# A Mamba, attention and mixture-of-experts block: one scan for both tiles of a second chunk, a convolution on one engine, and the last attention in two halves

## The chip, the cores and the metric

The kernel runs on one core of a Trainium2 chip. A core has five engines that run side by side, each through its own instructions in order: PE (TensorE, matrix products), DVE (VectorE), ACT (ScalarE), POOL (GpSimd) and SP (SyncE, which here only issues DMAs). DMA queues move data between HBM and the core's memory. The metric is the device time of one execution in microseconds; the median of several executions is compared.

## The reference

The input is x of shape 8 x 256 x 32 x 32: 8 batches of 1024 tokens with 256 channels. Cut to what matters here, layer 0 is this, with layer norms and residual additions around it:

```python
xm, z = split(xn @ W_in)                    # 512 channels each
xm = silu(causal_conv(xm, conv_w, 4 taps) + conv_b)
dt, Bm, Cm = split(xm @ W_x)
dt = softplus(dt @ W_dt + b_dt)             # [tokens, 512]
A = -exp(A_log)                             # [512, 16 states]
for t in tokens:                            # h: [512, 16]
    h = exp(dt[t] * A) * h + (dt[t] * xm[t]) * Bm[t]
    y[t] = sum over states of h * Cm[t]
y = (y + xm * D_param) * silu(z)
x = x + y @ W_out
x = x + gelu(layernorm(x) @ W1 + b1) @ W2 + b2
```

Layer 1 is attention with 8 heads of 32 channels over the 1024 tokens of a batch, with a bias per key column and head, and then a mixture of experts: the mean of a batch's tokens is routed, its two best of 8 experts (256 to 512 to 256 channels with GELU) are applied to all its tokens and added with weights, and a layer norm follows.

## The kernel before

**Tiles and steps.** A batch has two chunks of 512 tokens, 16 chunks in all. In a chunk the 512 inner channels are four tiles of 128 partitions, taken as two halves of two tiles each. The recurrence runs along the free dimension: for one state and one tile of channels, the scan instruction computes h over 512 tokens from the decays da_all and the inputs hb. A chunk has 16 states x 2 halves = 32 steps; the whole kernel has 512, walked by one loop (L2239). Each step g has four parts, all of them written by hand into the order of the engines' queues:

- `decay` (L891): ACT writes exp(dt * A) for both tiles into da_all, which has two buffers, two steps ahead.
- `inputs` (L908): DVE multiplies dt * xm with the row B, broadcast over partitions (tile bc), into a slot of the set h4 (tile hb), one step ahead. There are 4 slots; from a point in the run, when the weight w_z is no longer needed, its memory is a fifth (L958).
- `scan` (L920): DVE runs the recurrence over hb in place.
- `sums` (L943): DVE multiplies hb with the row C in place, and POOL issues a DMA that adds hb to the half's sum dx in memory (512 KB). The next step that adds to the same dx comes two steps later, and POOL waits for the earlier addition to land.

In the first chunk of a batch (c = 0) one scan instruction runs through both tiles as one row of 1024 elements; the decay of the second tile's first token is zero, so that nothing carries over. After it, POOL copies the last h of both tiles into the tile state. In the second chunk (c = 1) there are two scan instructions of 512 elements, one per tile, which start from the column of state as an operand; the two exponentials for two steps ahead follow one behind each of them.

**The other work** is written as Python generators, which a model of the engines' queues (L60 to L137) resumes when its clock says that their inputs are ready: `advance` (L2129) gives each due stream its turn by the order in URGENT, and where PE would stand idle it emits filler matmuls into unused memory (tile warm). The model's costs are constants in `vec_cost`, `act_cost`, `pe_cost`, `pool_cost`. The streams are:

- `prologue` (L685), the next chunk's xm, dt and dx: the convolution runs on DVE as three operations xm<-xp per tile, or, where CONV is set (chunks 3, 4 and 13), on PE as 16 products cv<-xp per tile; softplus adds its terms by DVE (e<-u) or, where SOFT is set, by POOL's DMAs into dt. FRONT gives the step at which it starts, GATE that of the gate z (`gate_part`, L991).
- `epilogue` (L1039), what follows a chunk's scans: gate, output product, FFN.
- `attention` (L1540), one batch at a time, in 32 units of 4 heads, 512 queries and 128 keys: scores (sc) on PE, exp (pt) on ACT, products with the values (num) on PE. The sum over keys (den) is a PE product too, except in the last batch, where DVE adds pt into the tiles dsum. The last batch's attention needs both chunks, so it starts when the last epilogue has ended.
- `route` (L1717) and `experts` (L1790): a batch's routing, small DVE operations, then indirect DMAs of the chosen experts' weights, issued by POOL (tile g), and the experts' products he and re.

All engine instructions are recorded by one helper, so that in the profile they have the line L98, and all DMAs L95. Operations are told apart by their tiles.

Of the kernel before, what the change touches and what calls it, by code (L numbers as in the profile page):

```python
# [54 lines left out]
def hybrid_kernel(ctx: ExitStack, tc: tile.TileContext, a: dict, out: bass.AP):  # L55
# [46 lines left out]
    def vec_cost(op, out, *ins):  # L102
        n, into = width(out), str(out)
        chained = op == "scalar_tensor_tensor" and vec.into == into
        vec.into = into
        if op == "tensor_tensor_scan":
            return (0.125 if n == CH else 0.07) + n * 2.08e-3
        return (0.2 if n < P else 0.065) + n * 1.04e-3 + 0.2 * chained
# [42 lines left out]
    w_z = load("w_z", [P, KC, DI], a["W_in"].rearrange("(k p) n -> p k n", p=P)[:, :, DI:])  # L151
# [69 lines left out]
    taps = const.tile([P, ND * KW, HD], F32, name="taps")  # L221
# [17 lines left out]
    base1 = const.tile([P, KC], F32, name="base1")  # L239
    base2 = const.tile([P, NF], F32, name="base2")  # L240
# [31 lines left out]
    FRONT = (7, 13, 4, 4, 1, 14, 10, 1, 13, 1, 10, 6, 1, 5, 10)  # L272
    GATE = (20, 4, 30, 30, 22, 7, 30, 18, 28, 25, 5, 28, 30, 30, 12, 26)
    CONV = (0, 0, 0, 1, 1, 0, 0, 0, 0, 0, 0, 0, 0, 1, 0, 0)
    SOFT = (1, 0, 0, 1, 0, 0, 0, 0, 1, 0, 1, 0, 0, 0, 0, 0)
# [274 lines left out]
    set_up, gates_ready, centered_w = [], [], []  # L550
# [43 lines left out]
    def conv_pe(i, xn, mem):  # L594


        c = i % NCH
        while not set_up:
            yield POLL
        xm, xp, ps, ps2 = [], None, None, None  # L600
        for d in range(ND + 1):
            if d < ND:
                if d % 2 == 0:
                    xm.append((yield from mem.take(f"xm_{i}_{d // 2}")))

                ps2 = yield from banks.take(f"xin_{i}_{d}")
                for k in range(KC):
                    pe.matmul(
                        ps2, w_in[:, k, d * P : (d + 1) * P], xn[:, k, :],
                        start=(k == 0), stop=(k == KC - 1),  # L610
                    )
            if d:
                for t in range(KW):
                    for r in range(4):
                        rows = slice(HD * r, HD * r + HD)
                        pe.matmul(
                            ps[rows, :], taps[rows, (d - 1) * KW + t, :], xp[rows, t : t + CH],
                            start=(t == 0), stop=(t == KW - 1),
                        )
                if c < NCH - 1:  # L620
                    act.copy(conv_tail[:, c + 1, d - 1, :], xp[:, CH:])
            yield
            if d:
                h, q = divmod(d - 1, 2)
                act.activation(xm[h][:, q, :], ps, AF.Identity, bias=V("conv_b", d - 1))
                banks.put(ps)
            if d < ND:
                xp = work_pool.tile([P, KW - 1 + CH], F32, name=f"xp_{i}_{d}", tag="xp", bufs=2)
                act.activation(xp[:, KW - 1 :], ps2, AF.Identity, bias=b_in[:, d : d + 1])
                act.copy(xp[:, : KW - 1], conv_tail[:, c, d, :])  # L630
                ps = ps2
            yield
        return xm

    def conv_parked(i, mem):
# [5 lines left out]
        for h in range(NHALF):  # L641
# [11 lines left out]
            if CONV[i]:  # L653
                for q in range(2):
                    d = 2 * h + q
                    ps = yield from banks.take(f"cv_{i}_{d}")
                    for t in range(KW):
                        for r in range(4):
                            rows = slice(HD * r, HD * r + HD)
                            pe.matmul(  # L660
                                ps[rows, :], taps[rows, d * KW + t, :], xps[q][rows, t : t + CH],
                                start=(t == 0), stop=(t == KW - 1),
                            )
                    yield
                    act.activation(xm[h][:, q, :], ps, AF.Identity, bias=V("conv_b", d))
                    banks.put(ps)
                continue
# [17 lines left out]
    def prologue(i: int):  # L685
# [6 lines left out]
        if i < PARK:  # L692
            xn = yield from mem.take(f"xn_{i}")
            yield sp.dma_start(xn, x_v[b, :, :, c * CH : (c + 1) * CH])
            xn = yield from layernorm(mem, banks, xn, xn, f"a{i}", kept=i)
            yield
            me["xn_d"] = dram.tile([P, KC, CH], F32, name=f"xn_d_{i}", tag=f"xn_d_{i}")
            stored = sp.dma_start(me["xn_d"], xn)
            xm = yield from (conv_pe if CONV[i] else conv_dve)(i, xn, mem)
            mem.put(xn, at=max(stored, model.end))  # L700
        else:
            xm = yield from conv_parked(i, mem)
# [6 lines left out]
        def skip_path():  # L709

            for h in range(NHALF):
                dx = me["acc", h] = yield from mem.take(f"dx_{i}_{h}")
                for r in range(2):
                    act.activation(
                        dx[:, r, :], xm[h][:, r, :], AF.Identity, scale=V("D", 2 * h + r)
                    )
# [159 lines left out]
    das, bcs, hbs = {}, {}, {}  # L876
# [14 lines left out]
    def decay(g, q):  # L891
        i, s, h = place(g)
        da = da_all[:, g % 2, q, :]
# [3 lines left out]
        skip = 1 if q and i % NCH == 0 else 0  # L897
        if skip and g % NSTEP < 2:
            act.copy(da[:, :1], zero_c)
        act.activation(  # L900
            da[:, skip:], chunk[i]["dt"][h][:, q, skip:], AF.Exp, scale=neg_a[:, n : n + 1]
        )
# [5 lines left out]
    def inputs(g):  # L908
# [5 lines left out]
        vec.at = max(vec.at, landed)  # L914
        xd = chunk[i]["xd"][h]
        vec.tensor_tensor(hb, xd, bc[:, 0, :].unsqueeze(1).to_broadcast([P, 2, CH]), ALU.mult)
# [3 lines left out]
    def scan(g, q):  # L920

        i, s, h = place(g)
        c = i % NCH
        hb = hbs[g]
        d = 2 * h + q
        done = das.pop((g, q))
        vec.at = max(vec.at, done)
        if c == 0:
            if q:
                both = hb.rearrange("p a t -> p (a t)")  # L930
                vec.tensor_tensor_scan(
                    both, da_all[:, g % 2].rearrange("p a t -> p (a t)"), both, 0.0,
                    ALU.mult, ALU.add,
                )
        else:
            vec.tensor_tensor_scan(
                hb[:, q, :], da_all[:, g % 2, q, :], hb[:, q, :], state[:, s, d : d + 1],
                ALU.mult, ALU.add,
            )
        if q and c < NCH - 1:  # L940
            pool.tensor_copy(state[:, s, 2 * h : 2 * h + 2], hb[:, :, CH - 1])

    def sums(g):  # L943
# [6 lines left out]
        y = hb[:, :, :n]  # L950
        vec.tensor_tensor(y, y, bc[:, 1, :n].unsqueeze(1).to_broadcast([P, 2, n]), ALU.mult)
        model.t = vec.at
        me["landed", h] = pool.dma_start(out=me["acc", h], in_=hb, accum_op=ALU.add)
# [4 lines left out]
    def park():  # L958
# [29 lines left out]
        h4.make = lambda nm, k: w_z if k == H4 else make(nm, k)  # L988
# [50 lines left out]
    def epilogue(i: int):  # L1039
# [20 lines left out]
        for h in range(NHALF):  # L1060
            yield me["landed", h]
            if c < NCH - 1:
                vec.tensor_tensor(
                    me["acc", h][:, :, CH - 1], me["dx_end"][:, 0, h], me["dx_end"][:, 1, h],
                    ALU.add,
                )
            vec.tensor_tensor(y[h], me["acc", h], y[h], ALU.mult)
# [348 lines left out]
    def center():  # L1416
# [17 lines left out]
        for n in range(E * F // (4 * P)):  # L1434
# [3 lines left out]
            mean = work_pool.tile([P, 4], F32, name=f"eW2_m_{n}", tag="r_rows1", bufs=1)  # L1438
# [11 lines left out]
    def expert_constants(pl):  # L1450
        vec.memset(loads_e, 0.0)
        for dst, n, step, mul, add in (
            (rev_e, E, 1, -1.0, float(E)), (base1, KC, P, 1.0, float(E * C)),
            (base2, NF, P, 1.0, float(E * F)),
# [85 lines left out]
    def attention(b: int):  # L1540

        last = b == B - 1
        mem = Owner(t4, 10, 0, NCH + 1) if last else Owner(t4, 6, 0, NCH)
        tn = [chunk[b * NCH + c]["tn"] for c in range(NCH)]
        dsums = []  # L1550
        if last:
            x1 = []
            for c in range(NCH - 1):
                x1.append((yield from mem.take(f"x1l_{c}")))
                sp.dma_start(x1[c], x1_d[b][c])
            x1.append(chunk[b * NCH + NCH - 1]["x1"])
        v = work_pool.tile([P, NT, C], F32, name=f"v_{b}", tag="v")
        for c in range(NCH):
            ps = yield from pairs.take(f"vp_{b}_{c}")
            for q in range(4):  # L1560
                for k in range(KC):
                    pe.matmul(
                        ps[:, q // 2, q % 2 * C : q % 2 * C + C],
                        tn[c][:, k, q * P : (q + 1) * P], wv[:, k, :],
                        start=(k == 0), stop=(k == KC - 1),
                    )
            yield
            vec.tensor_tensor(
                v[:, 4 * c : 4 * c + 4, :].rearrange("p j (h d) -> p j h d", d=HD),
                ps.rearrange("p a (j h d) -> p (a j) h d", h=NH, d=HD),  # L1570
                ecb[:, 4 * c : 4 * c + 4, :].unsqueeze(3).to_broadcast([P, 4, NH, HD]), ALU.mult,
            )
            pairs.put(ps)

# [29 lines left out]
        if last:  # L1604
            for n in range(2):
                dsums.append((yield from mem.take(f"dsum_{n}")))
# [3 lines left out]
        def products(g, c, j, pts):  # L1610
# [5 lines left out]
            for den in range(2):  # L1616
                for r in range(4):
                    h = 4 * g + r
                    if den and last:
# [925 lines left out]
```

## Time and profile before

| what | value |
|---|---|
| median of 5 runs | 3412.2 us (3400.8 to 3417.2) |
| the profiled execution's own time | 3405.1 us |
| its span, first to last instruction | 3403.3 us |
| mean granted clock of PE | 0.961 |
| DVE idle between first and last scan | 141 us of 2954 |
| scan instructions on DVE | 225 + 31 of 1024 elements, 448 + 64 of 512 |
| DMA, mean over the span | 196 GB/s; 8 or 9 tenths busy in most slices of the scan loop |
| dx<-hb, issue to landing | 4.4 / 7.7 / 14.5 us (least, median, most) |

A row of the groups gives line, engine, operation, output<-inputs by the program's names, shapes and count; then busy time and mean ns of one; then the idle time of the engine just before such instructions, and who ended it. In a row of the timeline the first number is the start in us from the span's start, the second the duration. Where several equal instructions follow each other, the timeline shows them as one (x2), and the duration is that of all. An instruction can begin before the one ahead of it on the same engine has ended, so that the distance between two starts says more of a cost than the duration.

### The profile page before, as it was taken

How to read it: one execution, taken by the hardware profiler on the slowest of the kernel's cores; microseconds unless marked ns; L12 is line 12 of the kernel's file. 1: busy time of each engine (PE TensorE's matmuls, PEld its weight loads, DVE VectorE, ACT ScalarE, POOL GpSimd, SP SyncE). 2: the span in 40 equal slices, each digit the busy share in tenths (PEclk: the TensorE clock that was granted, in tenths of full speed). 3: DMA queues.
4: the chain of work that ended last, by engine and by line, in shares of the span. 5: the costliest groups of instructions: out<-in, count | busy, mean ns of one | idle time of the engine just before them, and what ended most of it. 6: DMA issues, size and time to landing. Idle time of an engine off the chain costs nothing. (4 is left out here: it accounts for less than half of the span.)

```text
span 3403.3 us, 44585 instructions
## 1 busy us (share of the span) xinstructions
PE 3145.9 (92%) x16359; PEld 1391.5 (41%) x16359; DVE 2993.8 (88%) x3140; ACT 2466.5 (72%) x3610; POOL 1088.1 (32%) x1072
## 2 busy tenths in 40 slices
PE   8888988999899999999999899999899989999998
PEld 5544443433343334333443344333443343334343
DVE  6989999999989979899989999999999999962561
ACT  4666756678867888687778777787768878864643
POOL 0242134312432235334353245233542353221010
PEclk8989999999999999999999999999999999999999
DMA  4877989989988798889998999799998998972140
GB/s 122 240 197 190 222 214 218 235 205 232 218 212 236 192 216 198 214 208 219 227 244 187 229 226 214 184 215 222 218 240 195 232 220 195 216 170 75 38 97 23
DMA packets 216134, 668.21 MB, mean 196 GB/s; under 512 B 31200, under 2 KB 42592, under 8 KB 215904
## 3 DMA queue, kind: packets, MB, share of 16 engines
q0 software_dynamic: 106112, 373.88, 56.4%
q1 hardware_dynamic: 109792, 291.38, 25.2%
q8 instruction: 130, 2.13, 0.2%
q14 instruction: 100, 0.82, 0.1%
HBM read 269.20 MB, written 92.93 MB: 106 GB/s over the span
## 5 line engine op out<-in xcount | busy, mean ns | idle before, releaser
L98 ACT ACTIVATE da_all<-dt,vecs 128x512 f32<-128x512 f32 (+1 forms) x1024 | 699.6, 717 | 291.1 <-DVE hb L98 247.4
L95 POOL DMA_DIRECT2D dx<-hb x449 | 397.7, 891 | 1379.6 <-DVE hb L98 957.6
L98 DVE TENSOR_TENSOR hb<-xm,bc 128x1024 f32<-128x1024 f32 x449 | 540.5, 1204 | 23.5 <-issue 19.8
L98 DVE TENSOR_TENSOR_SCAN hb<-da_all,state,hb 128x512 f32<-128x512 f32 x448 | 553.1, 1269 | 3.8 <-ACT da_all L98 3.7
L98 ACT ACTIVATE pt<-sc 128x1024 f32<-128x1024 f32 x512 | 494.5, 1018 | 80.1 <-PE sc L98 69.4
L98 DVE TENSOR_TENSOR hb<-hb,bc 128x1022 f32<-128x1022 f32 (+1 forms) x449 | 546.6, 1217 | 0.0
L98 DVE TENSOR_TENSOR_SCAN hb<-da_all,hb 128x1024 f32<-128x1024 f32 x225 | 514.3, 2286 | 8.9 <-ACT da_all L98 8.9
L98 PE MATMUL warm<-mean_c,zero_c 128*128 128x256 f32 x1182 | 374.9, 442 | 49.8 <-ACT z L98 12.7
L98 POOL COPY state<-hb 128x2 f32<-128x2 f32 x225 | 321.0, 1427 | 209.7 <-DVE hb L98 204.6
L98 PE MATMUL sc<-qk,qk 32*128 32x512 f32 x2048 | 336.2, 646 | 21.1 <-ACT pt L98 18.7
L98 PEld LDWEIGHTS warm<-mean_c,zero_c 128*128 128x128 f32 x1182 | 225.6, 211 | 195.2 <-PE warm L98 74.0
L98 PE MATMUL num<-pt,v 128*32 128x512 f32 x2048 | 281.8, 620 | 14.2 <-DVE ot L98 14.2
L98 PE MATMUL den<-pt,ecb 128*32 128x512 f32 x1792 | 239.4, 605 | 0.0
L98 PE MATMUL facc<-fh,w 128*128 128x512 f32 x512 | 233.5, 602 | 5.5 <-ACT pt L98 2.2
L98 PE MATMUL re<-he,g 128*128 128x512 f32 x472 | 219.2, 609 | 19.9 <-ACT sz L98 7.8
L98 PE MATMUL fh<-x_f,w 128*128 128x512 f32 x480 | 228.7, 608 | 7.0 <-DVE x_f L98 2.3
L98 PE MATMUL he<-xe,g 128*128 128x512 f32 x448 | 217.7, 611 | 5.3 <-issue 3.7
L98 ACT ACT_TABLE_LOAD x159 | 204.0, 1283 | 3.5 <-PEq L2532 0.7
L98 PEld LDWEIGHTS sc<-qk,qk 32*128 32x128 f32 x2048 | 99.7, 184 | 200.8 <-ACT pt L98 83.1
L98 PEld LDWEIGHTS facc<-fh,w 128*128 128x128 f32 x512 | 95.4, 192 | 131.4 <-issue 118.2
L98 PEld LDWEIGHTS re<-he,g 128*128 128x128 f32 x472 | 89.4, 195 | 133.5 <-issue 100.8
L98 PEld LDWEIGHTS fh<-x_f,w 128*128 128x128 f32 x480 | 86.9, 191 | 134.6 <-issue 101.8
(422 smaller groups left out, 4697.8 us busy)
## 6 DMA issues: line engine op xcount, KB each, us to landing
dx<-hb POOLq DMA_DIRECT2D x449, 512.0 KB, 7.7
bc<-bc_d SPq DMA_DIRECT2D x256, 512.0 KB
dx<-w_z POOLq DMA_DIRECT2D x63, 512.0 KB, 7.2
dt<-e POOLq DMA_DIRECT2D x36, 512.0 KB, 11.1
dt<-u POOLq DMA_DIRECT2D x30, 512.0 KB, 11.2
xin_d<-z SPq DMA_DIRECT2D x28, 512.0 KB
sz_d<-z SPq DMA_DIRECT2D x28, 512.0 KB
sz<-sz_d SPq DMA_DIRECT2D x28, 512.0 KB
```

The lines of the kernel that those rows point to most:

```text
L95: f(*args, **kw)
L98: return f(*args, **kw)
```

## The change

**Scan.** A slot now has two rows of 513 elements; column 0 holds the state with which the row begins. da_all has the same form, with zeros in column 0, so one instruction of 1026 elements, from an initial value of 0, runs through both rows in both kinds of chunk. In second chunks POOL copies the state into the column; in first chunks POOL clears it, where the slot's column isn't zero already. The inputs' multiply doesn't touch the column. Both exponentials now follow the joined scan. The tile dx has 1026 elements, and the adding DMA carries 1025 of them (the second row's column lies between the two rows).

```diff
     def decay(g, q):
-        da = da_all[:, g % 2, q, :]
+        da = da_all[:, g % 2, q, 1:]
...
-        skip = 1 if q and i % NCH == 0 else 0
-        if skip and g % NSTEP < 2:
-            act.copy(da[:, :1], zero_c)
-        act.activation(
-            da[:, skip:], chunk[i]["dt"][h][:, q, skip:], AF.Exp, scale=neg_a[:, n : n + 1]
-        )
+        act.activation(da, chunk[i]["dt"][h][:, q, :], AF.Exp, scale=neg_a[:, n : n + 1])
...
     def inputs(g):
...
+        if i % NCH:
+            pool.at = max(pool.at, vec.at)
+            pool.tensor_copy(hb[:, :, 0], state[:, s, 2 * h : 2 * h + 2])
+            das[g, 2] = pool.at + 0.3
+            clean.discard(id(hb))
+        elif id(hb) not in clean:
+            pool.at = max(pool.at, vec.at)
+            pool.memset(hb[:, :, 0], 0.0)
+            das[g, 2] = pool.at + 0.3
+            clean.add(id(hb))
         xd = chunk[i]["xd"][h]
-        vec.tensor_tensor(hb, xd, bc[:, 0, :].unsqueeze(1).to_broadcast([P, 2, CH]), ALU.mult)
+        vec.tensor_tensor(
+            hb[:, :, 1:], xd, bc[:, 0, :].unsqueeze(1).to_broadcast([P, 2, CH]), ALU.mult
+        )
...
-    def scan(g, q):
+    def scan(g):
...
+        for q in range(3):
+            vec.at = max(vec.at, das.pop((g, q), 0.0))
+        vec.tensor_tensor_scan(
+            flat(hb), flat(da_all[:, g % 2]), flat(hb), 0.0, ALU.mult, ALU.add
+        )
+        if i % NCH < NCH - 1:
+            pool.tensor_copy(state[:, s, 2 * h : 2 * h + 2], hb[:, :, CH])
...
     def sums(g):
...
-        me["landed", h] = pool.dma_start(out=me["acc", h], in_=hb, accum_op=ALU.add)
+        me["landed", h] = pool.dma_start(
+            out=me["acc", h][:, 1:], in_=flat(hb)[:, 1:], accum_op=ALU.add
+        )
...
-            for q in range(2):
-                scan(now, q)
-                advance()
-                if now + 2 < nsteps and (q or i % NCH):
-                    for r in range(0 if i % NCH == 0 else q, q + 1):
-                        decay(now + 2, r)
+            scan(now)
+            advance()
+            if now + 2 < nsteps:
+                for q in range(2):
+                    decay(now + 2, q)
```

**Convolution, softplus, tables.** `conv_pe`, CONV, the diagonal weights taps and their setup are gone: every chunk convolves on DVE. Two more chunks that count have SOFT set (9 and 15). FRONT and GATE have new values, and `vec_cost` has new constants, so streams fall on other steps.

```diff
-        return (0.2 if n < P else 0.065) + n * 1.04e-3 + 0.2 * chained
+        if op == "tensor_reduce":
+            n = max(n, width(ins[0]))
+        if out.dtype == BF16 and n > CH:
+            return 0.1 + n * 0.535e-3
+        own = 0.2 if n < P else 0.31 if n == P else 0.065
+        if op == "scalar_tensor_tensor" and n == CH:
+            own = 0.13
+        return own + n * 1.04e-3 + 0.2 * chained
...
-    FRONT = (7, 13, 4, 4, 1, 14, 10, 1, 13, 1, 10, 6, 1, 5, 10)
-    GATE = (20, 4, 30, 30, 22, 7, 30, 18, 28, 25, 5, 28, 30, 30, 12, 26)
-    CONV = (0, 0, 0, 1, 1, 0, 0, 0, 0, 0, 0, 0, 0, 1, 0, 0)
-    SOFT = (1, 0, 0, 1, 0, 0, 0, 0, 1, 0, 1, 0, 0, 0, 0, 0)
+    FRONT = (7, 8, 4, 4, 1, 15, 10, 1, 13, 3, 8, 1, 8, 1, 14)
+    GATE = (20, 13, 30, 30, 26, 6, 27, 26, 30, 20, 7, 30, 17, 27, 28, 18)
+    SOFT = (1, 0, 0, 1, 0, 0, 0, 0, 1, 1, 1, 0, 0, 0, 0, 1)
```

**Last attention.** The last batch has a stream of its own, `attention_last`, with an urgency between those of the epilogue and the projections. It makes the values, queries and keys of chunk 14 when that chunk's epilogue has ended, and runs the 8 units of first-half queries and first-half keys; when the last epilogue has ended, it makes those of chunk 15 and runs the other 24. It has four dsum tiles instead of two. The parts that it shares with `attention` have become functions with the same operations (`values`, `scores_of`, `raise_scores`, `quotient`).

```diff
+        yield from operands(0)
+        for n in range(2 * NG):
+            dsums.append((yield from mem.take(f"dsum_{n}")))
+        yield from run_units([(g, 0, j) for g in range(NG) for j in range(NT // 2)])
+        while ("e", b * NCH + 1) not in done:
+            yield POLL
...
+        yield from operands(1)
+        yield from run_units(
+            [(g, 0, j) for g in range(NG) for j in range(NT // 2, NT)]
+            + [(g, 1, j) for g in range(NG) for j in range(NT)]
+        )
```

**Routing.** The row numbers of both weight matrices are computed together (two operations instead of four), and the biases of both layers are picked together:

```diff
         for k in range(2):
-            for rows, base, size, n in ((rows1, base1, C, KC), (rows2, base2, F, NF)):
-                vec.scalar_tensor_tensor(
-                    rows[:, k], first[:, k : k + 1].to_broadcast([P, n]), -float(size), base,
-                    ALU.mult, ALU.add,
-                )
+            vec.scalar_tensor_tensor(
+                rows[:, k], sizes, first[:, k : k + 1], bases, ALU.mult, ALU.add
+            )
...
             for k in range(2):
-                for dst, src, n in ((hbias, "eb1", NF), (obias, "eb2", KC)):
-                    vec.tensor_tensor(
-                        t[:, :n], V(src).rearrange("p (n e) -> p n e", e=E),
-                        oh[:, k].unsqueeze(1).to_broadcast([P, n, E]), ALU.mult,
-                    )
-                    vec.tensor_reduce(dst[:, k], t[:, :n], AX.X, ALU.add)
-                vec.tensor_scalar(obias[:, k], obias[:, k], w2e[:, k : k + 1], None, ALU.mult)
+                vec.tensor_tensor(
+                    t[:, k], eb, oh[:, k].unsqueeze(1).to_broadcast([P, NF + KC, E]), ALU.mult
+                )
+            vec.tensor_reduce(ebias, t, AX.X, ALU.add)
+            vec.tensor_tensor(
+                ebias[:, :, NF:], ebias[:, :, NF:],
+                w2e.unsqueeze(2).to_broadcast([P, 2, KC]), ALU.mult,
+            )
```

## The prediction

> **What bounds the kernel now.** I read the page's first two sections, then busy time by stage, then the groups of instructions, then single steps in the timeline. The page alone would mislead: it puts PE at 92% and DVE at 88%, so PE looks like the bound.
>
> ```profile
> PE 3145.9 (92%) x16359; PEld 1391.5 (41%) x16359; DVE 2993.8 (88%) x3140; ACT 2466.5 (72%) x3610; POOL 1088.1 (32%) x1072
> ```
>
> By stage (columns: PE, PEld, DVE, ACT, POOL busy, clock, DMA share, GB/s) it is otherwise. The lines are the scan loop (first to last scan), one first chunk, one second chunk, then three pieces of the tail:
>
> ```profile
> 72.00:3026.00 2954.00, 2736.85 (x14383) 1193.93 (x14378) 2812.89 (x2789) 2253.40 (x3322) 1049.24 (x1019) 0.96 0.90 215
> 2322.10:2502.00 179.90, 157.56 (x775) 73.25 (x768) 168.01 (x163) 120.08 (x180) 87.55 (x85) 0.95 0.97 227
> 2502.00:2679.20 177.20, 173.25 (x932) 65.16 (x932) 172.72 (x168) 154.71 (x216) 53.24 (x50) 1.00 0.90 208
> 3026.00:3130.00 104.00, 101.15 (x525) 50.76 (x518) 22.75 (x62) 44.66 (x67) 15.20 (x16) 1.00 0.38 100
> 3130.00:3286.00 156.00, 154.83 (x846) 57.52 (x844) 96.79 (x154) 103.69 (x122) 9.15 (x9) 1.00 0.25 55
> 3286.00:3403.00 117.00, 96.92 (x353) 51.65 (x352) 22.47 (x68) 33.85 (x50) 12.83 (x13) 0.96 0.14 42
> ```
>
> In the loop DVE is busy 2812.9 of 2954 us. Of PE's 2736.9, 310 are filler matmuls (tile warm), which leaves it 82% of real work. So the loop's 2954 us go by DVE's work plus its 141 us of idle time. The last 378 us have no scans; there PE is busy 353 us, 40 of them 142 filler matmuls, and idle 25.
>
> **Part 1, the joined scan.** The groups (mean ns of one after "busy,"):
>
> ```profile
> L98 DVE TENSOR_TENSOR_SCAN hb<-da_all,state,hb 128x512 f32<-128x512 f32 x448 | 553.1, 1269 | 3.8 <-ACT da_all L98 3.7
> L98 DVE TENSOR_TENSOR_SCAN hb<-da_all,hb 128x1024 f32<-128x1024 f32 x225 | 514.3, 2286 | 8.9 <-ACT da_all L98 8.9
> L98 DVE SCALAR_TENSOR_TENSOR xm<-xp,vecs,xm 128x512 f32<-128x512 f32 x156 | 105.5, 744 | 7.4 <-ACT xm L98 7.4
> ```
>
> By these means a pair costs 2x1269-2286 = 252 ns more than one joined scan, 64 us over 256 steps. But durations overlap, so I read whole steps, a second chunk's and a first chunk's:
>
> ```profile
> 2519.34 2.45 DVE L98 TENSOR_TENSOR_SCAN hb<-da_all,state,hb 128x512 f32<-128x512 f32 x2
> 2521.72 1.20 DVE L98 TENSOR_TENSOR hb<-xm,bc 128x1024 f32<-128x1024 f32 x1
> 2522.83 1.21 DVE L98 TENSOR_TENSOR hb<-hb,bc 128x1024 f32<-128x1024 f32 x1
> 2523.97 2.45 DVE L98 TENSOR_TENSOR_SCAN hb<-da_all,state,hb 128x512 f32<-128x512 f32 x2
> ```
> ```profile
> 2354.16 2.28 DVE L98 TENSOR_TENSOR_SCAN hb<-da_all,hb 128x1024 f32<-128x1024 f32 x1
> 2356.36 1.20 DVE L98 TENSOR_TENSOR hb<-xm,bc 128x1024 f32<-128x1024 f32 x1
> 2356.58 1.03 POOL L98 COPY state<-hb 128x2 f32<-128x2 f32 x1 [1.18 <-DVE hb L98]
> 2357.48 1.22 DVE L98 TENSOR_TENSOR hb<-hb,bc 128x1022 f32<-128x1022 f32 x1
> 2358.61 2.28 DVE L98 TENSOR_TENSOR_SCAN hb<-da_all,hb 128x1024 f32<-128x1024 f32 x1
> ```
>
> The pair takes 2521.72-2519.34 = 2.38 us of DVE, the joined scan 2356.36-2354.16 = 2.20. That is 0.18 x 256 = 46 us saved. Two more elements at 2286/1024 = 2.2 ns in all 512 steps return 2.3. **-44 us.** The joined scan also waits for both exponentials at once: 256 joined scans waited 9.9 us for ACT (8.9, and 1.0 for tile w_z), 512 halves 3.8. **+6 us.**
>
> **The new wait.** Each second-chunk scan now waits for a POOL copy of its state (256 of them), which stands on POOL behind the dx<-hb DMA of two steps earlier, and that waits for an earlier dx DMA to land. The trace has the mirrored copy, state<-hb: 180 ns at the least, median 1029, at most 5502 (above: 1.03 beside a multiply of 1.20, ending with it). DVE loses nothing to it in the step shown: its starts lie 2.20, 1.12 and 1.13 apart. Normally the copy ends 2 to 3 us before its scan. I looked up, for each second-chunk step of this trace, the end of the POOL instruction behind which the changed program puts the copy: about 24 of 256 would have been late, by 50 us in sum, or some 33 when neighbours share one delay. What delays it:
>
> ```profile
> 1830.89 1.78 POOL L95 DMA_INDIRECT g<-in_eW,rows  x1 [0.30 <-issue]
> 1842.11 1.40 POOL L95 DMA_INDIRECT g<-eW_d,rows  x1 [0.30 <-issue]
> 1843.51 1.94 POOL L95 DMA_DIRECT2D dx<-hb  x2
> ...
> POOL dx L95 <- DMA dx<-hb: 231.1, 65, 10.4
> ```
>
> Six expert gathers block POOL for 12.6 us here, and 65 waits for dx landings sum to 231 us. The shifted order of streams moves these places, and DVE has 57 us of idle in second chunks that some delay fills. Bounds 0 and +50; I take **+16**, nearer to the row in which DVE loses nothing. The 37 memsets for first chunks have no waiter before the next scan: 0.
>
> [...]
>
> **Part 2, convolution off PE.** Three chunks go from PE to DVE: 12 tiles of 3 taps, 36 more xm<-xp operations. By the mean 744 that is 26.8; six in a row take 4.04 us in the timeline, so 36 x 0.67 = **+24 us** of DVE. PE loses 192 matmuls (cv<-xp, 43.4 us busy), which buys nothing where DVE is the bound. ACT trades 12 x 0.67 for 12 x 0.80: nothing, it is 76% busy. The setup's taps, five small DVE operations: -1.
>
> **Part 3, softplus sums.** Two chunks more add by DMA: four e<-u operations of 1.25 leave DVE, **-5**. Four dt<-e DMAs (0.83 to 2.1 us of POOL) and 4 x 1.05 of ACT come; both lie beside DVE.
>
> **Part 4, routing.** Per route, two row operations go (0.15 each), and ten of 194, 178, 186, 170 and 256 ns (two of each, 1.97 us) become four of about 0.2: -1.4 us. Six routes in the loop: **-8**.
>
> **Part 5, the tail.** The last attention's first half starts before the last chunk's operands, so 8 of its 32 units can run beside the last epilogue. In program order 863 matmuls stand after the last scan against 891, and all 28 fewer are fillers. A filler there costs between 40/142 = 0.28 us (busy) and (40+25)/142 = 0.46 with the tail's PE idle: 8 to 13 us. Bounds 0 (PE is 97% busy from 3026 to 3130, and every real matmul remains) and -25; I take **-12**, and -1 for the last route.
>
> **Part 6, order and DMA.** New start tables move prologues and gates; their worth is some part of DVE's 141 us idle, bounds -20 and +20, taken as 0. The accumulating DMA moves 4100 instead of 4096 bytes per partition, 0.1%: 0. [...]
>
> **Sum** against the profiled execution's own 3405.1 (span 3403.3): -44+6+16+24-1-5-8-13 = -25, so **3380 us**. The median of the five runs, 3412.2, is 7 higher (0.2%); what a measurement of this kernel can tell from no change is about 0.3%, 10 us.
>
> **Rivals.**
> 1. *Larger gain* (0.22): the copies are never late and the tail yields its 25: -44+6+24-14-26 = -54, and part of the idle with it: 3325 to 3355. For it: the copy's slack of 2 to 3 us. Against: the gathers above.
> 2. *No gain* (0.10): the loop's saving returns as DVE idle. PE has 82% real work and DMA 0.97 in the first chunk shown, so streams that finish no sooner hold the next chunk: 3395 to 3415.
> 3. *Slower, by the copy* (0.18): POOL's queue becomes the loop. Its place is the scan of second chunks, its price the delay of the copy. It decides once the copies cost 16+25 = 41 us, 0.16 us per step: dx landings (median 7.7, longest 14.5) past about 11 us, which use up the slack, do it. At 0.3 us per step, 77 us: 3441. For it: the 231 us of POOL waits. Against: DVE waited 3.2 us for dx landings.
>
> My forecast, 3355 to 3395, has 0.50. Range 3328 to 3422: it takes in the late copies at +50, the tail at nothing, and most of rival 1. Faster 0.71, same 0.10, slower 0.19.
>
> **What would show it.** Second-chunk steps of 4.45 us between scan starts instead of 4.62; 192 xm operations; DVE busy in the loop 44-24+14 = 34 us lower; a new DVE wait on POOL for hb of 10 to 50 us, at gathers and dx landings; about 28 fewer fillers in a tail of some 365 us. The forecast is wrong if that wait exceeds 50, if DVE idle grows elsewhere, or if the tail holds 378.

## The result and the profile after

The changed kernel takes 3415.0 us (median of 44 runs), the kernel before 3404.8 (median of 86): ratio 1.0025, 95% interval [1.0016, 1.0035]. The forecast was 3380, a ratio of 0.9926 to the profiled execution that it started from. The change is no gain, and a small loss that lies within the 0.3% which the forecast called no change. The profiled execution has a span of 3414.9 us, 11.6 more than before. First the page's busy times, then the scan loop and the tail (columns as before):

```profile
PE 3153.5 (92%) x16047; PEld 1399.8 (41%) x16047; DVE 2963.8 (87%) x2847; ACT 2459.6 (72%) x3598; POOL 1262.0 (37%) x1373
```
```profile
77.00:3047.30 2970.30, 2751.27 (x13999) 1206.74 (x13999) 2780.36 (x2507) 2247.13 (x3311) 1223.19 (x1317) 0.96 0.91 215
3047.40:3414.90 367.50, 342.28 (x1662) 152.57 (x1658) 140.09 (x267) 181.54 (x238) 36.60 (x38) 0.97 0.26 65
```

The loop has 282 fewer DVE instructions, and DVE is busy 2780 us in it instead of 2813, and yet the loop is longer. A steady second-chunk step is what the forecast said, 1481.87 - 1477.42 = 4.45 us against 4.62:

```profile
1477.42 2.28 DVE L98 TENSOR_TENSOR_SCAN h<-da_all,h 128x1026 f32<-128x1026 f32 x1
1479.62 1.19 DVE L98 TENSOR_TENSOR h<-xm,bc 128x1024 f32<-128x1024 f32 x1
1480.74 1.21 DVE L98 TENSOR_TENSOR h<-h,bc 128x1024 f32<-128x1024 f32 x1
1481.87 2.28 DVE L98 TENSOR_TENSOR_SCAN h<-da_all,h 128x1026 f32<-128x1026 f32 x1
```

The groups and DVE's waits tell where it went (a group's last part is the idle time before it; a wait's numbers are us in sum, times, longest):

```profile
L98 DVE TENSOR_TENSOR_SCAN h<-da_all,h 128x1026 f32<-128x1026 f32 x449 | 1027.2, 2288 | 50.1 <-ACT da_all L98 32.3 <-POOL h L98 15.3
L98 DVE TENSOR_TENSOR_SCAN w_z<-da_all,w_z 128x1026 f32<-128x1026 f32 x63 | 144.1, 2288 | 17.2 <-POOL w_z L98 16.1 <-ACT da_all L98 1.0
L98 DVE SCALAR_TENSOR_TENSOR xm<-xp,vecs,xm 128x512 f32<-128x512 f32 x192 | 130.1, 743 | 14.5 <-ACT xm L98 14.5
```
```profile
DVE h L98 <- ACT da_all L98: 32.3, 16, 5.5
DVE w_z L98 <- POOL w_z L98: 16.1, 4, 6.2
DVE h L98 <- POOL h L98: 15.3, 9, 6.1
```

Scans stood still for 14 us before and for 65 now: 31.4 of it for POOL, in 13 scans (28.7 in eleven for copies, 2.7 in two for memsets), and 33.3 for ACT's exponentials instead of 13.6. From the two traces I summed DVE's idle time between the first and the last scan by the kind of operation that it stands ahead of:

| us | before | after |
|---|---|---|
| DVE busy in the loop | 2811.7 | 2779.2 |
| idle ahead of scans | 13.7 | 67.2 |
| idle ahead of the inputs' multiplies | 25.9 | 3.3 |
| idle ahead of the streams' operations | 100.0 | 118.3 |
| start to first scan | 71.9 | 76.9 |
| last scan to end | 380.1 | 369.9 |

A late copy in the trace, on DVE and on POOL. The scan at 1492.56 could have started at 1486.3; its copy is queued behind a DMA that itself waited for DVE, and behind six gathers that the routing put there (the first POOL line is the copy of the step before, which was in time):

```profile
1485.20 1.21 DVE L98 TENSOR_TENSOR h<-h,bc 128x1024 f32<-128x1024 f32 x1
1492.56 2.30 DVE L98 TENSOR_TENSOR_SCAN w_z<-da_all,w_z 128x1026 f32<-128x1026 f32 x1 [6.15 <-POOL w_z L98]
```
```profile
1478.57 1.11 POOL L98 COPY h<-state 128x2 f32<-128x2 f32 x1
1482.48 0.86 POOL L95 DMA_DIRECT2D dx<-h  x1 [2.80 <-DVE h L98]
1483.64 1.38 POOL L95 DMA_INDIRECT g<-in_eW,rows  x1 [0.30 <-issue]
...
1491.37 0.95 POOL L95 DMA_INDIRECT g<-eW_d,rows  x1 [0.30 <-issue]
1492.32 0.20 POOL L98 COPY w_z<-state 128x2 f32<-128x2 f32 x1
```

Three scans stood behind such a row of gathers, for 6.1 us each: 18.4 of the 28.7.

### The profile page after: what moved, and what is told of

It is laid out like the page before. It is cut to its first block, busy times and chain, and to the rows that moved or that the text cites. A ratio compares the mean times of both kernels' runs of the same rounds, so it can differ in the third digit from the quotient of the medians.

```text
span 3414.9 us, 43870 instructions
## 1 busy us (share of the span) xinstructions
PE 3153.5 (92%) x16047; PEld 1399.8 (41%) x16047; DVE 2963.8 (87%) x2847; ACT 2459.6 (72%) x3598; POOL 1262.0 (37%) x1373
## 3 DMA queue, kind: packets, MB, share of 16 engines
q0 software_dynamic: 106688, 376.24, 56.9%
## 5 line engine op out<-in xcount | busy, mean ns | idle before, releaser
L98 DVE TENSOR_TENSOR_SCAN h<-da_all,h 128x1026 f32<-128x1026 f32 x449 | 1027.2, 2288 | 50.1 <-ACT da_all L98 32.3
L98 ACT ACTIVATE da_all<-dt,vecs 128x512 f32<-128x512 f32 x1024 | 680.0, 716 | 315.7 <-DVE h L98 264.1
L95 POOL DMA_DIRECT2D dx<-h x449 | 397.2, 886 | 1197.0 <-DVE h L98 564.7
L98 DVE TENSOR_TENSOR h<-h,bc 128x1022 f32<-128x1022 f32 (+1 forms) x449 | 546.6, 1217 | 0.0
L98 DVE TENSOR_TENSOR h<-xm,bc 128x1024 f32<-128x1024 f32 x449 | 540.8, 1204 | 3.3 <-DMA dx<-h 3.2
L98 PE MATMUL warm<-mean_c,zero_c 128*128 128x256 f32 x1238 | 413.9, 453 | 69.8 <-ACT dt L98 15.8
L98 POOL COPY state<-h 128x2 f32<-128x2 f32 x225 | 293.9, 1314 | 236.1 <-DVE h L98 216.4
L98 POOL COPY h<-state 128x2 f32<-128x2 f32 x224 | 278.3, 1242 | 0.0
L98 DVE TENSOR_TENSOR_SCAN w_z<-da_all,w_z 128x1026 f32<-128x1026 f32 x63 | 144.1, 2288 | 17.2 <-POOL w_z L98 16.1
L98 DVE SCALAR_TENSOR_TENSOR xm<-xp,vecs,xm 128x512 f32<-128x512 f32 x192 | 130.1, 743 | 14.5 <-ACT xm L98 14.5
```

Source lines behind the costliest of these rows:

```text
L95: f(*args, **kw)
L98: return f(*args, **kw)
```

## The experiments

Two theories. **W**: the joined scan's own waits (POOL's copies, ACT's exponentials) ate what it saved. **L**: the work is in a written order that fits the times of one kernel; another order costs, and waits show only where it does. Most experiments on the changed kernel keep the order in which the streams' work stands on every engine: only the instruction in question is exchanged, and the planner is charged as if nothing had happened. "Against the changed kernel" below is the difference of the two ratios to before, times 3405 us; by the intervals of the two ratios it is good to some 6 to 9 us either way.

**Two scans again, in the changed kernel's order.**

```diff
-            pool.tensor_copy(hb[:, :, 0], state[:, s, 2 * h : 2 * h + 2])
+            model.do(pool, 1.2)
...
+            for q in range(2):
+                vec.engine.tensor_tensor_scan(
+                    hb[:, q, 1:], da_all[:, g % 2, q, 1:], hb[:, q, 1:],
+                    state[:, s, 2 * h + q : 2 * h + q + 1], ALU.mult, ALU.add,
+                )
```

> The changed kernel with the order of all streams kept, but second chunks scan the two tiles one after the other from the state operand, and nothing copies the state into the column. Theory W: DVE works 45 us more, the 31 us of waits for POOL and 10 to 20 of those for ACT go; the time stays within 10 us of the changed kernel, ratio to before 1.000 to 1.006. Theory L: the waits are only displaced, so the 45 us come on top: ratio 1.012 to 1.016.

Measured: ratio 0.9997 [0.9983, 1.0012], 10 us faster than the changed kernel. In the loop DVE is busy 38 us more and idle 40 less, so the loops of the two profiled executions differ by only 2 us; of the other 6 us of their spans 4 lie ahead of the first scan and 2 in the tail. At the place of the late copy the scans start on time, and the waits for ACT are 22.8 us (L897 is the line of the exchanged scan):

```profile
1480.11 1.22 DVE L98 TENSOR_TENSOR h<-h,bc 128x1024 f32<-128x1024 f32 x1
1481.25 2.46 DVE L897 TENSOR_TENSOR_SCAN w_z<-da_all,state,w_z 128x512 f32<-128x512 f32 x2
```
```profile
DVE h L98 <- ACT da_all L98: 17.8, 6, 5.8
DVE h L897 <- ACT da_all L98: 5.0, 4, 2.7
```

What the joined scan saves, its waits take: it costs between 2 us (the loops) and 10 us (the times), and the 22 that were forecast for it are not there either way. W holds for this part.

One thing stands beside all comparisons with the changed kernel. PE's granted clock has a median of 0.958 in the changed kernel's executions, and of 0.961 in those with two scans and in those of the kernel before that were measured beside the experiments (0.960 to 0.963 in the next two variants and in the one without the moved operations). By the line given in the last section, 0.003 of clock goes with some 7 us. Whether the clock makes the time, or both follow from something else, no run separates.

**The joined scan without the copies.**

```diff
-            pool.tensor_copy(hb[:, :, 0], state[:, s, 2 * h : 2 * h + 2])
+            model.do(pool, 1.2)
```

> The changed kernel in its own order, without the 256 copies of the state into the slots' columns: second chunks start from zero, so the state that the first chunk leaves is left out. [...] Theory W: the 31 us of waits for POOL go and nothing takes their place: 25 to 40 us faster than the changed kernel, ratio to before 0.991 to 0.996. Theory L (waits only move): within 10 us of the changed kernel, ratio 0.999 to 1.005.

Measured: 0.9944 [0.9926, 0.9961], 28 us faster than the changed kernel. That is the copies' price in this order; in the profiles the loop is 24 us shorter. Against the two scans it is 18 us (0.9997 - 0.9944), of the 40 that DVE is spared (2817.5 us busy in the loop with two scans, 2777.0 here). The other half went to waits for ACT: scans waited 35.4 us for it against 22.8, and all of DVE's operations together 78.9 us against 58.9 (gaps over 0.15 us). Of these waits:

```profile
DVE h L98 <- ACT da_all L98: 33.5, 17, 5.8
```

**The copies queued one DMA earlier on POOL.**

```diff
+        ahead(g + 2)     # takes the slot and queues its copy
         me["landed", h] = pool.dma_start(
             out=me["acc", h][:, 1:], in_=flat(hb)[:, 1:], accum_op=ALU.add
         )
```

> The changed kernel in its own order, but the copy of the state for a second chunk's step is queued on POOL one DMA earlier: ahead of the dx DMA of two steps before instead of behind it, and ahead of all that the streams issue on POOL in between. Theory W: most of the 31 us of waits for POOL go (those behind gathers and behind waiting dx DMAs); 15 to 28 us faster than the changed kernel, ratio to before 0.994 to 0.998. If the copies are late because of work that stands before both places: 0 to 8 us faster.

Measured: 0.9975 [0.9954, 0.9995], 17 us faster than the changed kernel, and faster than both kernels. The scans' waits for POOL fall from 31.4 to 9.6 us, 7.1 of them for copies into h (L899 is the copy's line):

```profile
DVE h L98 <- ACT da_all L98: 28.8, 15, 5.2
DVE h L98 <- POOL h L899: 7.1, 3, 3.7
```

Most copies were late because of what stood between these two places in POOL's queue, and it was not the copy's own time.

**The copies on ACT.**

```diff
-            pool.tensor_copy(hb[:, :, 0], state[:, s, 2 * h : 2 * h + 2])
+            model.do(pool, 1.2)
+            act.engine.copy(hb[:, :, 0], state[:, s, 2 * h : 2 * h + 2])
```

> The changed kernel with the order of all streams kept, but the copy of the state into the slot's column is done by ACT instead of POOL in second chunks. Theory W (the loop lost its gain to the joined scan's new waits, 31 us for POOL's copies and about 20 more for ACT): the waits for POOL go, ACT gets 256 x 0.19 = 49 us of work at 72% busy, of which up to 10 us come back as waits; 20 to 30 us faster than the changed kernel, some 3390, ratio to before 0.994 to 0.997. Theory L (the streams' new order is what costs; waits only show where it shows up): other waits take their place, within 6 us of the changed kernel, ratio 1.001 to 1.004.

Measured: 1.0268 [1.0250, 1.0286], 83 us slower than the changed kernel. Neither theory foresaw it. The copies take 180 ns each on ACT, but they stand behind two exponentials and whatever else ACT has, and 57 scans wait for them:

```profile
DVE h L98 <- ACT h L874: 112.2, 49, 5.7
...
DVE w_z L98 <- ACT w_z L874: 14.4, 8, 4.4
```

**The exponentials straight behind the scan.**

```diff
             scan(now)
+            if now + 2 < nsteps:
+                for q in range(2):
+                    decay(now + 2, q, now=True)     # queued here, charged below
             advance()
```

> The changed kernel in its own order on all engines but ACT, where the two exponentials for the step after next are queued straight behind the scan, ahead of what the streams issue during it. Theory W (the exponentials come late behind streams' work): DVE's waits of 33 us for da_all fall to 10 or less: 10 to 20 us faster than the changed kernel, ratio to before 0.996 to 1.000. Rival: ACT then stands still until the scan has ended, up to 2.2 us per step, and the streams' work behind it comes late: 20 us slower or more.

Measured: 1.0488 [1.0466, 1.0511], 158 us slower than the changed kernel. The rival was right, and too small. Waits for da_all fell only to 21 us. ACT stands still until the scan ends: ACT's own waits, the changed kernel's first, then this one's:

```profile
ACT da_all L98 <- DVE h L98: 264.1, 156, 10.4
```
```profile
ACT da_all L859 <- DVE h L98: 517.2, 253, 10.3
```

The streams' ACT work behind it came late, and DVE's idle time ahead of streams' operations rose from 106 to 266 us (gaps over 0.15 us).

**Without the moved convolution's operations.**

```diff
+                    if i in (3, 4, 13):
+                        model.do(vec, vec_cost("scalar_tensor_tensor", y))
+                        continue
                     vec.scalar_tensor_tensor(
```

> The changed kernel in its own order, without the 36 DVE operations xm<-xp of chunks 3, 4 and 13, those that were PE's work before; three of four taps of these chunks are left out. It is the price of the moved convolution on DVE alone. The forecast's step (DVE bounds the loop): 20 to 26 us faster than the changed kernel, ratio to before 0.994 to 0.997. Rival (it lies in DVE's idle time of those chunks): less than 8 us faster.

Measured: 0.9992 [0.9977, 1.0007], 11 us faster than the changed kernel, between the step's 20 to 26 and the rival's 8. DVE is spared 23.2 us in the three chunks in which these operations stand; the chunks are shorter by 4.1, 0.2 and 7.6, the rest became idle time.

**The last attention in one piece** (the function of the kernel before, for the last batch).

```diff
-            start(attention_last(B - 1), ("l",), model.t)
+            yield from attention_old(B - 1)
```

> The changed kernel with the last batch's attention as before, in one piece after the last epilogue. If the two halves are what shortened the tail, the stretch after the last scan is 367 us again 378: 10 us slower than the changed kernel, ratio to before 1.004 to 1.007. If the tail was shortened by something else (fewer fillers by the new order), within 4 us of the changed kernel.

Measured: 1.0104 [1.0085, 1.0122], 27 us slower than the changed kernel, more than either expectation. The stretch after the last scan is 384 us instead of 367.5. The two halves do shorten the tail, by 17 us; the other 10 us are not explained.

```profile
3039.10:3423.40 384.30, 358.19 (x1742) 164.15 (x1738) 139.81 (x267) 182.08 (x238) 36.73 (x38) 0.99 0.25 62
```

**Other orders of the changed kernel.** Each of these changes when the planner starts streams, or what it thinks they cost; the work is the same. The old FRONT and GATE:

> The changed kernel with FRONT and GATE of the kernel before. Theory L (the order of the streams is what costs): the time moves by 15 us or more, down if the old tables suit better. Theory W (the joined scan's waits cost): the waits for POOL stay between 20 and 45 us, and the time stays within 10 us of the changed kernel, ratio to before 1.000 to 1.006.

The old constants of vec_cost:

> The changed kernel with the constants of vec_cost of the kernel before; FRONT and GATE stay new. Theory L: the first scan starts some 5 us earlier again (the setup's order was changed by the constants), and chunk 0 loses its 17 us of extra idle time: 10 to 25 us faster than the changed kernel, ratio to before 0.995 to 1.000. Theory W: within 10 us of the changed kernel, ratio 1.000 to 1.006.

The gathers two at a time:

```diff
+            yield model.t + 4.0
             for i in range(NF):
                 pool.indirect_dma_start(
...
+                if i % 2:
+                    yield model.t + 4.0
```

> The changed kernel with the six expert gathers of a batch's first six experts pairs issued two at a time, 4 us apart, instead of in one row. Theory W: three waits for POOL of 6.1 us each, and part of the rest, fall to 2 us or less: 8 to 16 us faster than the changed kernel, ratio to before 0.998 to 1.000. Theory L: the order after it shifts, by up to 10 us either way, and the sum of DVE's idle time stays within 10 us of 190.

One start moved by one step, twice:

```diff
-    FRONT = (7, 8, 4, 4, 1, 15, 10, 1, 13, 3, 8, 1, 8, 1, 14)
+    FRONT = (7, 8, 4, 4, 1, 14, 10, 1, 13, 3, 8, 1, 8, 1, 14)
```

> The changed kernel with one start moved: the sixth chunk's successor begins its prologue at step 14 instead of 15. Theory L (any order that was not searched for costs some tens of us): 15 to 70 us slower than the changed kernel, ratio to before 1.007 to 1.023. Rival (only the whole set of old values is bad): within 10 us of the changed kernel, ratio 1.000 to 1.006.

```diff
-    FRONT = (7, 8, 4, 4, 1, 15, 10, 1, 13, 3, 8, 1, 8, 1, 14)
+    FRONT = (7, 9, 4, 4, 1, 15, 10, 1, 13, 3, 8, 1, 8, 1, 14)
```

> The changed kernel with another start moved: the second chunk's successor begins its prologue at step 9 instead of 8, so that nearly the whole order after it differs. Theory L: 15 to 70 us slower than the changed kernel, ratio to before 1.007 to 1.023. Rival: within 10 us of the changed kernel, ratio 1.000 to 1.006.

| order | ratio to before | against the changed kernel |
|---|---|---|
| old tables | 1.0221 [1.0205, 1.0236] | +67 us |
| old costs | 1.0217 [1.0202, 1.0233] | +65 |
| gathers apart | 1.0201 [1.0177, 1.0225] | +60 |
| sixth start one step earlier | 1.0173 [1.0151, 1.0195] | +50 |
| second start one step later | 1.0278 [1.0255, 1.0301] | +86 |

All five lose 50 to 86 us; of the two starts moved by a single step, one loses least and the other most. Neither theory foresaw the loss with the old costs or with the gathers apart, and of the single steps one lies within L's 15 to 70 us and one above. DVE's work is the same in all of them (2777 to 2786 us in the loop); its idle time is 240 to 279 us instead of 189, and most of the rise stands ahead of the streams' operations. When the gathers stood apart, the scans' waits for POOL did fall to 15 us, and the time rose all the same. That another order costs, L's main point, is shown five times. That the new start values were fitted to this one program, and the old ones to theirs, is what I infer from it; no run shows how they were chosen.

**The kernel before with one part of the change.** All convolutions on DVE:

```diff
-    CONV = (0, 0, 0, 1, 1, 0, 0, 0, 0, 0, 0, 0, 0, 1, 0, 0)
+    CONV = (0,) * 16
```

> The kernel before with all chunks' convolutions on DVE, nothing else changed. If DVE bounds the loop, as the forecast says, 36 more operations cost 24 us: ratio 1.006 to 1.009. If the chunks concerned had DVE idle time that takes it (rival), 0 to 10 us: ratio 1.000 to 1.003.

Measured: 1.0207 [1.0186, 1.0227], 70 us. DVE has 24 us more work in the loop, as expected, and 46 us more idle time, which neither expectation had and which I put down to the changed order; so this run can't price the part. Beside it the joined scan with the planner's knowledge:

> The kernel before with the joined scan alone (slots of 513, copies by POOL), old tables, old costs, old attention and routing; the convolution is all on DVE, since its PE weights and the wider slots don't fit in memory together. To be compared with the kernel before that has only the convolution moved. Theory W: DVE works 44 us less and waits 35 to 50 more for POOL and ACT: within 10 us of that kernel. The forecast's sum (waits of 22): 22 us faster than that kernel. Theory L: no such waits with the old order, 35 to 44 us faster than that kernel, ratio to before 0.993 to 0.998.

Measured: 1.0294 [1.0280, 1.0308], 30 us more than the former. That none of the three expectations gave, and it is no price of the scan either: its order is yet another.

The joined scan in the old order, with nothing told to the planner; both exponentials of a second chunk's step now follow it, as in the changed kernel. PE's convolution weights stay in memory here, dx keeps its 1024 elements, and the adding DMA takes a row in two pieces of 512 elements (2 KB):

```diff
-            vec.tensor_tensor_scan(
-                hb[:, q, :], da_all[:, g % 2, q, :], hb[:, q, :], state[:, s, d : d + 1],
-                ALU.mult, ALU.add,
-            )
+            model.do(vec, vec_cost("tensor_tensor_scan", hb[:, q, 1:]))
+        if q:
+            vec.engine.tensor_tensor_scan(
+                flat(hb), flat(da_all[:, g % 2]), flat(hb), 0.0, ALU.mult, ALU.add
+            )
...
-        me["landed", h] = pool.dma_start(out=me["acc", h], in_=hb, accum_op=ALU.add)
+        me["landed", h] = pool.dma_start(out=me["acc", h], in_=hb[:, :, 1:], accum_op=ALU.add)
```

> The kernel before in its own order of streams on all engines (the planner's costs untouched), with the joined scan of 513-element rows in second chunks and the copies on POOL where the changed kernel has them; the adding DMA takes a row in two pieces of 512. The forecast's sum for this part, -44+6+16: 22 us faster than before, ratio 0.993. Theory W (waits of 40 us eat the 38 us, as in the changed kernel's order): within 8 us of before, ratio 0.998 to 1.002.

With the copies one DMA earlier:

> The same with the copies queued on POOL one DMA earlier. In the changed kernel that took the waits for POOL from 31 to 7 us and 16 us off the time. Theory W: 12 to 25 us faster than before, ratio 0.993 to 0.9965. If the old order has other late copies, or the adding DMA in pieces lands later: within 8 us of the run with the copies late.

With the pieces alone, and two scans:

> The kernel before in its own order with slots of two rows of 513 whose first column isn't used, two scans in second chunks as before, and the adding DMA in two pieces of 512 elements per partition. It is the price of the pieces (and of the wider slots) alone. If the copies are what cost in the old order (theory W): within 10 us of before, ratio 0.998 to 1.003. If the pieces are (rival): 30 us slower or more, ratio above 1.008.

And without the copies:

> The same with the joined scan in second chunks, without the copies: the state that the first chunk leaves is left out. Theory W: DVE's 34 us come back and no copy is waited for, 15 to 30 us faster than the pieces alone, ratio to before 0.990 to 0.998. Theory L (this order fits the two scans' times, and any change of them costs): no faster than the pieces alone, ratio 1.000 or more.

| in the old order | ratio to before | DVE busy, idle in the loop |
|---|---|---|
| pieces alone, two scans | 1.0067 [1.0046, 1.0088] | 2815, 170 us |
| joined scan, copies late | 1.0161 [1.0138, 1.0184] | 2778, 234 |
| joined scan, copies early | 1.0087 [1.0062, 1.0111] | 2775, 200 |
| joined scan, no copies | 1.0054 [1.0033, 1.0075] | 2776, 199 |

The pieces, with the wider slots that this run has too, cost 23 us, between the two expectations. Against them the late copies make the joined scan 32 us slower, early ones bring it within the intervals (+7), and without copies it is 4 us faster, within the intervals too (these differences are good to some 10 us). The run with late copies is slower than any expectation had it; the one with early copies lies between its two. So in the old order only some 4 of the scan's 40 us of DVE work come back, even where no copy is waited for: what L says. The profiles show 29 of the 40 as idle time (170 to 199 us); the profiled execution with the pieces alone was 20 us slower than its own median, which is why its row and its time don't agree better.

## Why the prediction was wrong

**What failed first: part 1's sum, -44+6+16 = -22.** Measured with the order kept, the joined scan costs 10 us by the times (1.0025 against 0.9997) and 2 by the loops of the profiles, a miss of 24 to 32, which is most of the whole miss (34: -25 forecast, some +9 measured). By its terms:

- -44, DVE's work: -38 (2817.5 to 2779.2 us busy in the loop). The step's reading was right, 4.45 against 4.62.
- +16, the copies: 28.7 us of waits (31.4 with the memsets, which were put at 0 and took 2.7), 28 us of time when they are left out. The mechanism was named and lay within the stated 0 to 50, and the POOL queue of the trace before had said 33. I went below it because "DVE has 57 us of idle in second chunks that some delay fills". It filled little: 28.7 of the 33 came, most of them at the gathers.
- +6, the exponentials: 20 us more waits for ACT in the profile (13.6 to 33.3), 10 of them by the exchange of the scan alone (22.8 to 33.3).

**What failed below it: "the loop's 2954 us go by DVE's work plus its 141 us of idle time", with the idle held fixed.** DVE is the busiest (2780 us of the loop's 2970 after the change, PE 2751), but work taken from it doesn't come back whole. Without copies 18 of 40 us came back; of the moved convolution 11 of 23; in the old order some 4 of 40. Without copies the rest came back as waits for ACT, in the old order as waits for ACT first. That the place of this work in the queues had been chosen for the longer time is my reading, not measured. The forecast itself named this as a sign of being wrong, "if DVE idle grows elsewhere", and it came: without the waits for POOL, DVE's idle time in the loop rose from 140 to 157 us.

**Part 2, +24:** 11. DVE does spend 23, but its idle time in the three chunks takes half. That error and the former are one: I applied a full price both where work went and where it came.

**Parts 3 and 4** were not priced alone. Parts 2 to 6 together were forecast at +24-1-5-8-13 = -3; the changed kernel with two scans stands at 0.9997 [0.9983, 1.0012], -1 us, but the errors in it cancel: with 11 instead of 24 for part 2 something else cost what I left out.

**Part 5, -12:** the tail is 10 us shorter (380.1 to 369.9). Fillers in it fell from 142 to 92. The step and its size were right against the kernel before; against the same kernel with the attention in one piece it is 17 us of tail.

**Part 6, the order, "taken as 0", bounds -20 and +20:** inside the loop the net was -4 (the inputs' waits -23, the streams' +18, with the new start values). The bounds were wrong in kind. The five other orders cost 50 to 86 us, so the range of this part had to be wider than that of any other, upward.

**Rival 3** named the right mechanism, the copy, but placed its turning point at 41 us of waits for POOL; with ACT's waits and the fixed idle time assumed away, 31 were enough. **Rival 2** gave the right time for a reason of which half is right: the saving did return as DVE's idle time.

**What stays open.** The first scan starts at 77 us instead of 72 in the changed kernel's profile. That is not the changed order by itself: DVE's operations up to there are the same in twelve profiles, and the first scan starts at 77 us in five of them (changed kernel, copies on ACT, no copies, old last attention, sixth start moved) and at 71 to 73 in the other seven. What goes with it is PE's granted clock between 26 and 40 us, 0.71 or 0.72 in the five and 1.00 in the seven; in that stretch PE's 16 products b_in, for which DVE waits, take 3.41 us in the five and 1.84 in the seven. The kernel before, whose DVE operations up to there are others, has the low clock too, 0.66 and 3.41 us, and its first scan at 72. Why an execution gets the one clock or the other is open. Why another order loses 50 us and not 10 was measured as waits of streams, not traced to one cause. A third da_all buffer, which could take ACT's wait away, wasn't tried.

The forecast put no work of DVE down to the copies: "DVE loses nothing to it in the step shown". That was right here: the step shown above, from 1477.42 with a POOL copy in it, has DVE starts 2.20, 1.12 and 1.13 apart, as before, and without the 256 copies DVE is busy only 2.2 us less in the loop (2777.0 against 2779.2). The copies themselves took 188 ns at the least and 1114 in the median, and the one in that step 1.11 us.

## What to carry to other kernels

In a kernel whose queues are written out for its own times, an engine's busy time is not a price list: work removed from the busiest engine came back to between a tenth and a half here, and each of five other orders of the same work cost 50 to 86 us, so exchange single instructions with the order held when a part is to be priced. A wait that joins two engines is priced by what is queued ahead of the releasing instruction: the same copy cost 28 us behind a DMA and some gathers, 11 (28 less the 17 regained) one DMA earlier, and 83 more on another engine with room to spare by its busy share. When the old trace says how late a new operation would have been, take that number, not the idle time that one hopes will cover it.

## What the runs showed of the hardware

- With an adding DMA of 512 KB in 2 KB pieces instead of 4 KB rows (the kernel before with the pieces alone) its queue's share of the 16 engines was 59.9% instead of 56.4%, its median landing 8.0 us instead of 7.7, and the time 23 us longer; the slots of that kernel were wider too, so the time is not the pieces' alone for certain. The changed kernel's rows of 4100 bytes, which start one element later in their tile, landed in 7.6 us in the median (share 56.9%): no cost seen.
- The same program's time goes with the clock that PE is granted: among the changed kernel's runs 3393.0 us at 0.966 and 3425.7 at 0.954, and a line through all of them falls 0.65% per 1% of clock, though DVE is the busiest engine of the loop (2780 us against PE's 2751). That the clock is the cause is not shown.
- The copy of a state into a slot (128x2 elements) takes 180 ns on ACT, and on POOL 0.19 us at the least, 1.1 in the median and 3.1 at most; the slower engine was the better place: with the copies on ACT the time was 83 us longer.
